# Attention and a routed feed-forward net on one core: zero products, logit sums, stores and GpSimd's multiplications in another order

## The chip, the cores and the metric

The kernel runs on one NeuronCore of a Trainium2 chip. A core has a matrix engine (TensorE, PE in the profile, with its weight loads as PEld), three engines for element-wise work (VectorE or DVE, ScalarE or ACT, GpSimd or POOL) and a queue that only issues transfers (SyncE, SP). Each engine works through its own list of instructions in order; between engines there are only waits on semaphores. TensorE writes into eight banks of PSUM, from which VectorE and ACT read. The metric is the time of one execution on the device in microseconds (us); a smaller one is better.

## The reference, cut to what matters

Sixteen sequences of 128 rows of 128 numbers attend to contexts of 77 rows (16 heads of 8). Then a net of four experts is applied four times; in each of these rounds every row is routed to its two best experts.

```python
x = x + tanh(g_xattn[0]) * xattn(layernorm(x), ctx_768, Wq, bq, Wkv, bkv, Wo, bo)
cur = layernorm(x)
for r in range(4):
    logits = cur @ Wg[r] + bg[r]
    vals, idx = top_k(logits, 2)
    cw = sum(one_hot(idx, 4) * softmax(vals)[..., None], axis=1)
    hmid = gelu(einsum('nh,ehf->enf', cur, W1) + b1[:, None, :])
    y = einsum('enf,efh->enh', hmid, W2) + b2[:, None, :]
    cur = cur + einsum('ne,enh->nh', cw, y)
x = x + tanh(g_ffn[0]) * cur
```

## The kernel before, in words

**Order.** TensorE, VectorE and ACT run in the order in which the program is written; so do GpSimd's instructions, which are pinned to it. Small lists of functions (`early`, `extra`, `behind` for each step of attention, `mid` and `post` for each piece of the experts) say between which others an instruction is put.

**PSUM.** `bank` gives one of two banks of a pool that most small products share; a new product waits until the tile that had its bank is read. `bank_tr` gives one of two others, `banks2` one of two pairs that hold the scores of a step. `warm(n)` multiplies zeros n times into a bank of `bank`; nothing reads the result.

**Attention** takes 16 steps, one for each sequence b. A step transposes the exponentials of its sequence (`turn_weights`, TensorE; ACT copies them out as `exT`), multiplies the scores of sequence b+1, has VectorE take their maximum and difference and ACT their exponential (`weights`), applies the output matrix for sequence b-1 (`put_out`, `ps_o`), takes statistics of its rows (`stats_x1`), and then (`attend`) multiplies `exT` by ones and by the values (`ps_av`) and has VectorE divide (reciprocal `rs`, product `oT`). `beats` keeps some of VectorE's instructions, so that others can be made to wait for one of them. GpSimd spreads the keys of later sequences (`km`) and norms rows.

**The rows are split in two halves** of eight tiles of 128 rows. While attention is at the second half, the first half is routed: its rows are transposed (`turned0`), the logits multiplied (`logits0`, `ps_lg`), the bias added and the gate worked out in steps (`gate0`, `gate`, one of them a Tanh on ACT), rows counted and placed (`counted0`, `routed0`, `placed0`). Then GpSimd stores the rows, tile by tile, each at its place by pair of experts (`scatter`, line 519), each store bound to one beat; SP loads them back, sorted (`load`, line 536). Line 973 says which store stands in which step.

**The turn to the experts.** In the last step `begin` copies the weights of the first four pieces (`bring`). After it stand four zero products, the transposes of the first sorted rows (`turn_half`, `ps_c`, copied to `curT`), four zero products, and the first phase, in which `put_last` finishes the last sequence.

**The experts** take eight phases: two halves in turn, four rounds. A phase has 21 pieces: two for each tile of a half, and five borders between tiles, between the fourth tile and the fifth. A piece multiplies the first layer into `ps_h`, ACT applies Gelu, and after the next piece's first layer the second layer is multiplied into `ps_y`; VectorE adds the weighted result to the rows (line 1090), and `sums` keeps these sums. VectorE also copies the weights of the piece four ahead to one of five buffers (`wb`, line 1000, 128x1028 numbers).

**The next round's routing** lies inside these phases. When a tile is finished, GpSimd multiplies its rows with the router's weights of all four experts (`multiply`, tile `lp`, four buffers), and VectorE sums (`sum_up`, line 417). In the other half's phase the last tile follows, then bias and gate up to `hot` (line 447), count (`ps_n`), places (`ps_pos`), eight stores, each bound to the latest sum of a piece, and the load. In the last two phases `finish` adds the residual to each tile and GpSimd stores it to the output (line 1098).

Of the kernel before, what the change touches and what calls it, by code (L numbers as in the profile page):

```python
# [46 lines left out]
def gated_xattn_moe(  # L47
# [358 lines left out]
    def multiply(h, r, t):  # L406

        prods[h, t] = work.tile([P, E, D], F32, tag="lp", name="lp", bufs=4)
        gp.tensor_tensor(
            prods[h, t], rows[h][:, t, 0:D].unsqueeze(1).to_broadcast([P, E, D]), wg_rows[:, r],  # L410
            ALU.mult,
        )

# [250 lines left out]
    def warm(n):  # L664

        ps = bank("ps_warm")
        for _ in range(n):
            mm(ps[:, :P], zero, zero, start=True, stop=True)
# [133 lines left out]
    def attend(b, exT):  # L802

        ps = bank("ps_av")
        for w in range(2):
            for k in range(HG):
                for g in range(NG):
                    at = slice(g * GW, (g + 1) * GW)  # L810
                    mm(
                        ps[at, ts(w, L)],
                        one[:, k, :] if w == 0
                        else vm[b // BB % 2][:, b % BB, k * D + g * GW : k * D + (g + 1) * GW],
                        exT[:, g * HG + k, :],
                        start=(k == 0),
                        stop=(k == HG - 1),
                    )
        rs = awork.tile([D, L], F32, tag="rs", name="rs")
        nc.vector.reciprocal(rs, ps[:, 0:L])  # L820
        oT = awork.tile([D, L], F32, tag="oT", name="oT")
        beats.append(nc.vector.tensor_tensor(oT, ps[:, ts(1, L)], rs, ALU.mult))
        return oT

    def put_out(b, oT, bank):
# [3 lines left out]
        nc.vector.scalar_tensor_tensor(  # L829
            row(b, D, D), ps[:, :D], tg[:, 0:1], x_sb[:, b, :],  # L830
            ALU.mult, ALU.add,
        )
# [76 lines left out]
    early = {b: [] for b in range(B)}  # L909
    behind = {b: [] for b in range(B)}  # L910
# [37 lines left out]
    def gate0(g):  # L948
        add_bg(0, 0, g, first["lg"])
        if g:  # L950
            first["gate"] = gate(0)
            advance(first["gate"], GATE_1)
# [15 lines left out]
    behind[7] += [lambda: logits0(0), lambda: gate0(0)]  # L968
    extra[9] += [lambda: turned0(1)]
    behind[9] += [lambda: logits0(1), lambda: gate0(1)]  # L970
    behind[10] += [counted0, lambda: advance(first["gate"])]
    behind[11] += [routed0, placed0, lambda: stored0(0)]
    stores_at = {(12, 0): 1, (12, 1): 2, (12, 2): 3, (13, 0): 4, (13, 1): 5, (13, 2): 6, (14, 0): 7}
# [40 lines left out]
    def begin():  # L1014
# [7 lines left out]
        junk = const.tile([1, 1], F32, name="junk")  # L1022
        nc.scalar.activation(junk, zero[0:1, 0:1], AF.Gelu_apprx_tanh)

    extra[B - 1] += [begin]
    o = {}
    for b in range(B):
# [22 lines left out]
        o[b] = attend(b, exT)  # L1050
# [4 lines left out]
        for k in range(3):  # L1055
            if (b, k) in stores_at:
                scatter(0, first["pos"], stores_at[b, k], stores, beats[n - 3 + k])
        if b == 14:
            load(0, stores)
# [51 lines left out]
    def phase(p, first_mid=()):  # L1111
# [33 lines left out]
        if ro < R:  # L1145
            s = 1 if p else 2

            if p:

                at(post, 0)(lambda: multiply(o, ro, NT - 1))  # L1150
# [74 lines left out]
        if r < R - 1:  # L1225

            for t, i, k in (
                (0, 13, 14), (1, 13, 15), (2, 14, 16), (3, 14, 17), (4, 15, 18), (5, 17, 19),  # L1230
                (6, 19, 20),
            ):
                at(post, i)(lambda t=t: multiply(h, r + 1, t))
                at(post, k)(lambda t=t: sum_up(h, t))

        for i, u in enumerate(units):
# [12 lines left out]
            def second(pc=pc, hT=hT, i=i, kind=u[0], k=u[1]):  # L1249
# [4 lines left out]
                if r == R - 1:  # L1254

                    n = i - NT - len(BORDERS)
                    if n in (0, 2, 4, 6):
                        finish(h, n // 2, id_i)
                    elif n in (1, 3, 5, 7):
                        finish(h, NT // 2 + n // 2, id_i)  # L1260
# [13 lines left out]
    warm(4)  # L1274
    turn_half(0, 0, state[0]["c"])
    warm(4)
# [36 lines left out]
```

## Time and profile before

| | us |
|---|---|
| three runs | 467.44, 467.48, 468.66 |
| their median | 467.48 |
| the profiled execution | 467.39 |
| its span in the trace | 465.60 |

| stretch of the span | from, to | length |
|---|---|---|
| start, up to the first transposes of exponentials | 0, 24.5 | 24.5 |
| attention | 24.5, 121.2 | 96.7 |
| first phase's `ps_b` to the second's | 147.12, 191.86 | 44.74 |
| each of the next five such stretches | 191.86, 395.10 | 40.64 or 40.65 |

`ps_b` is the product that brings in the second layer's bias, once in each phase; it serves as a mark.

In a row of a timeline stand the start, the length, the engine, the line of the program, the operation, what is written and from what, and the shape; "x8" means that eight instructions were merged, and a bracket at the end tells how long the engine had been idle and what ended it. A matrix product of this number type appears as two records. In a row of stretches each engine's busy time is followed by the number of its instructions in parentheses; the three last numbers are TensorE's granted clock as a share of full speed, the busy share of the transfer engines and GB/s.

### The profile page before, as it was taken

The numbers are of one execution on the slowest core, as the hardware profiler recorded it, in microseconds if no ns is written. First come the engines' busy times: TensorE is split into PE (matmuls) and PEld (weight loads), VectorE is DVE, ScalarE is ACT, GpSimd is POOL, SyncE is SP. The second block draws the span as 40 slices with busy tenths as digits, with TensorE's granted clock in tenths as the row PEclk, the third lists the DMA queues.
The fourth block names the chain that finished last, engine by engine and source line by source line (L and its number), as shares of the span: only waits on it lengthen the run. The fifth ranks groups of instructions, "written<-read, shape, count | busy, mean of one in ns | idle before, by whom it ended". The sixth has DMA issues, their size and how long they took to land.

```text
span 465.6 us, 12218 instructions
## 1 busy us (share of the span) xinstructions
PE 445.5 (96%) x4506; PEld 415.4 (89%) x4506; DVE 347.0 (75%) x900; ACT 275.0 (59%) x853; POOL 211.2 (45%) x249
## 2 busy tenths in 40 slices
PE   7999999989899899999999999999999999999991
PEld 6778888777799899999999999999999999999991
DVE  7259998989665998688579768857976885775551
ACT  2356776666555456566656656665665666566560
POOL 5354645227204732582366258236625924461042
PEclk8779999999999989999999999999999999999997
DMA  7420000002201400230121013012101301220000
GB/s 198 137 93 2 4 1 3 2 13 84 95 2 49 139 1 2 72 118 1 48 84 59 1 70 119 1 48 77 67 3 69 118 3 49 94 86 8 1 30 17
DMA packets 19553, 24.08 MB, mean 52 GB/s; under 512 B 3940, under 2 KB 16550, under 8 KB 19366
## 3 DMA queue, kind: packets, MB, share of 16 engines
q1 hardware_dynamic: 14868, 13.41, 9.1%
q0 software_dynamic: 3648, 9.71, 5.7%
q8 instruction: 36, 0.59, 0.5%
q10 hardware_dynamic: 978, 0.18, 0.2%
q14 instruction: 23, 0.19, 0.1%
HBM read 13.58 MB, written 9.71 MB: 50 GB/s over the span
## 4 chain that ended last, share of the span: by engine, by line
PE 81%; issue 7%; DVE 5%; POOL 3%; ACT 2%; POOLq 0%; DVEq 0%; ACTq 0%
PE ps_y L262 28%; PE ps_h L262 28%; PE ps_av L262 6%; PE ps_tr L265 6%; PE sc L262 2%; POOL out_dram L1098 2%; PE ps_warm L262 2%; PE ps_c L265 2%; PE ps_b L262 2%; DVE wb L1000 1%; PE ps_pos L262 1%; PE ps_o L262 1%; ACT exT L800 1%; DVE vm L197 1%; PE ps_q L262 1%
## 5 line engine op out<-in xcount | busy, mean ns | idle before, releaser
L1076 ACT ACTIVATE hT<-ps_h,wb 128x128 f32<-128x128 f32 x512 | 146.0, 368 | 87.9 <-ACT hT L1076 55.4
L262 PE MATMUL ps_h<-curT,wb 128*128 128x128 f32 x1024 | 136.3, 277 | 1.8 <-DVE wb L1000 1.8
L262 PE MATMUL ps_y<-wb,hT 128*128 128x128 f32 x1024 | 136.7, 277 | 0.0
L262 PEld LDWEIGHTS ps_h<-curT,wb 128*128 128x128 f32 x1024 | 125.5, 193 | 2.0 <-DVE wb L1000 2.0
L262 PEld LDWEIGHTS ps_y<-wb,hT 128*128 128x128 f32 x1024 | 125.4, 193 | 0.0
L519 POOL DMA_INDIRECT sorted<-rows,pos_i x64 | 69.6, 1087 | 116.5 <-DVE start L512 61.1
L1000 DVE COPY wb<-wall 128x1028 f32 x128 | 107.5, 842 | 11.7 <-issue 4.0
L93 POOL TENSOR_TENSOR lp<-rows,wg_rows 128x512 f32<-128x512 f32 x48 | 72.5, 1535 | 38.3 <-DVE rows L1090 31.4
L1090 DVE SCALAR_TENSOR_TENSOR rows<-ps_y,pws,rows 128x128 f32<-128x128 f32 x128 | 44.3, 346 | 36.2 <-PE ps_y L262 35.9
L1076 ACT ACTIVATE hT<-ps_h,wall 128x128 f32<-128x128 f32 x160 | 45.6, 368 | 35.9 <-PE ps_h L262 33.8
L800 ACT COPY exT<-ps_tr 77x512 f32<-77x512 f32 x64 | 34.1, 581 | 17.5 <-PE ps_tr L265 17.3
L262 PEld LDWEIGHTS ps_y<-wall,hT 128*128 128x128 f32 x320 | 38.9, 192 | 6.1 <-ACT hT L1076 6.1
L262 PE MATMUL ps_y<-wall,hT 128*128 128x128 f32 x320 | 43.1, 278 | 0.0
L262 PE MATMUL ps_h<-cx,wall 128*128 128x128 f32 x320 | 42.3, 275 | 0.0
L265 PEld LDWEIGHTS ps_tr<-ident,ex 128*77 128x77 f32 x256 | 29.5, 154 | 11.1 <-ACT exT L800 8.3
L262 PEld LDWEIGHTS ps_h<-cx,wall 128*128 128x128 f32 x320 | 39.0, 192 | 0.0
L265 PE MATMUL ps_tr<-ident,ex 128*77 128x128 f32 x256 | 36.8, 289 | 1.7 <-ACT exT L800 1.7
L417 DVE TENSOR_REDUCE lg<-lp 128x4 f32<-128x512 f32 x48 | 32.4, 675 | 5.5 <-POOL lp L93 5.5
L1098 POOL DMA_INDIRECT out_dram<-res,id_i x16 | 18.4, 1151 | 37.0 <-DVE res L1095 36.4
L782 DVE TENSOR_REDUCE mx<-sc 128x8 f32<-128x616 f32 x32 | 25.4, 792 | 11.8 <-PE sc L262 11.7
L792 ACT ACTIVATE ex<-ex 128x616 f32<-128x616 f32 x32 | 23.0, 719 | 10.9 <-DVE ex L786 10.4
L1090 DVE SCALAR_TENSOR_TENSOR rows<-ps_y,pwxs,rows 128x128 f32 x40 | 13.9, 348 | 17.0 <-PE ps_y L262 16.0
(162 smaller groups left out, 463.1 us busy)
## 6 DMA issues: line engine op xcount, KB each, us to landing
rows<-sorted SPq DMA_DIRECT2D x16, 528.0 KB
x_sb<-in_x_dram SPq DMA_DIRECT2D x4, 256.0 KB
wall<-in_L_ffn_W_dram SPq DMA_DIRECT2D x1, 1024.0 KB
wall<-in_L_ffn_W_dram SPq DMA_DIRECT2D x4, 256.0 KB
wg_rows<-wg_turned SPq DMA_DIRECT2D x1, 1024.0 KB
sorted<-rows,pos_i POOLq DMA_INDIRECT x64, 2.5
ctx_sb<-in_ctx_dram SPq DMA_DIRECT2D x4, 115.5 KB
out_dram<-res,id_i POOLq DMA_INDIRECT x16, 2.4
```

The costliest lines, as they stand in the source:

```text
L93: return lambda *a, **kw: tc.keep_in_program_order(f(*a, **kw))
L262: nc.tensor.matmul(*args, **kw)
L265: nc.tensor.transpose(*args)
L417: nc.vector.tensor_reduce(lgs[h][:, t, :], prods.pop((h, t)), AX.X, ALU.add)
L519: ins = nc.gpsimd.indirect_dma_start(out=sorted_rows[h], out_offset=bass.IndirectOffsetOnAxis(ap=pos_i[:, t : t + 1], axis=0), in_=rows[h] ...
L782: beats.append(nc.vector.tensor_reduce(mx, sv, AX.X, ALU.max))
L792: nc.scalar.activation(eu, eu, AF.Exp, scale=1.0 / math.sqrt(DH))
L800: nc.scalar.copy(exT[:, ts(g, HG), :].rearrange("m h l -> m (h l)"), ps[:M, :])
L1000: nc.vector.tensor_copy(wb, wall[:, ds(e, 1), :].rearrange("p o n -> p (o n)"))
L1076: nc.scalar.activation(hT[:, fc, :], ps[:, ts(fc, P)], AF.Gelu_apprx_tanh, bias=wb[:, W_B + fc : W_B + fc + 1],)
L1090: return nc.vector.scalar_tensor_tensor(at, y, w, at, ALU.mult, ALU.add)
L1098: ins = nc.gpsimd.indirect_dma_start(out=out_rows, out_offset=bass.IndirectOffsetOnAxis(ap=id_i[:, t : t + 1], axis=0), in_=res, in_offset ...
```

## The change

1. `warm` writes to a bank of the scores' pool instead of the common one.
2. `attend` is cut in two: after its products the functions of a new list `amid` run, then the division (`over_sums`). In steps 7 and 9 the routing logits and the adding of their bias are in `amid`, ahead of the division. The gate's Tanh goes from the end of step 10 to step 11, behind the copies of `exT`, and its last instruction to the end of step 11.
3. Stores of the first half: up to four in a step (VectorE's part of `put_out` becomes a beat too), so that all eight are issued by step 13, and the load one step earlier.
4. The first sorted rows are transposed in step 15 ahead of `attend`; the table for Gelu is loaded after that; the two groups of four zero products are left out.
5. Each of GpSimd's multiplications waits for the latest sum of a piece. They stand at pieces 13 to 19, one each, their sums two pieces later; the sum of the seventh tile comes in the first piece of the next phase.
6. The output stores of the last two phases stand in another order.

```diff
-    def multiply(h, r, t):
+    def multiply(h, r, t, behind):
         prods[h, t] = work.tile([P, E, D], F32, tag="lp", name="lp", bufs=4)
-        gp.tensor_tensor(
+        ins = gp.tensor_tensor(
             prods[h, t], rows[h][:, t, 0:D].unsqueeze(1).to_broadcast([P, E, D]), wg_rows[:, r],
             ALU.mult,
         )
+        after(ins, behind, "one tile for each piece of work")
...
-        ps = bank("ps_warm")
+        ps = banks2("ps_warm")
         for _ in range(n):
-            mm(ps[:, :P], zero, zero, start=True, stop=True)
+            mm(ps[:, 0, :P], zero, zero, start=True, stop=True)
...
+        return ps
+
+    def over_sums(ps):
         rs = awork.tile([D, L], F32, tag="rs", name="rs")
         nc.vector.reciprocal(rs, ps[:, 0:L])
...
-        nc.vector.scalar_tensor_tensor(
+        beats.append(nc.vector.scalar_tensor_tensor(
             row(b, D, D), ps[:, :D], tg[:, 0:1], x_sb[:, b, :],
             ALU.mult, ALU.add,
-        )
+        ))
...
-    def gate0(g):
+    def logits0_done(g):
         add_bg(0, 0, g, first["lg"])
-        if g:
-            first["gate"] = gate(0)
-            advance(first["gate"], GATE_1)
+
+    def gate0():
+        first["gate"] = gate(0)
+        advance(first["gate"], GATE_1)
...
-    behind[7] += [lambda: logits0(0), lambda: gate0(0)]
+    amid[7] += [lambda: logits0(0), lambda: logits0_done(0)]
     extra[9] += [lambda: turned0(1)]
-    behind[9] += [lambda: logits0(1), lambda: gate0(1)]
-    behind[10] += [counted0, lambda: advance(first["gate"])]
-    behind[11] += [routed0, placed0, lambda: stored0(0)]
-    stores_at = {(12, 0): 1, (12, 1): 2, (12, 2): 3, (13, 0): 4, (13, 1): 5, (13, 2): 6, (14, 0): 7}
+    amid[9] += [lambda: logits0(1), lambda: logits0_done(1)]
+    behind[9] += [gate0]
+    behind[10] += [counted0, lambda: advance(first["gate"], GATE_2 - GATE_1)]
+    extra[11] += [lambda: advance(first["gate"], 1)]
+    behind[11] += [lambda: advance(first["gate"]), routed0, placed0, lambda: stored0(0)]
+    stores_at = {
+        (12, 0): 1, (12, 1): 2, (12, 2): 3, (12, 3): 4, (13, 0): 5, (13, 1): 6, (13, 2): 7,
+    }
...
-        junk = const.tile([1, 1], F32, name="junk")
-        nc.scalar.activation(junk, zero[0:1, 0:1], AF.Gelu_apprx_tanh)
-
     extra[B - 1] += [begin]
...
-        o[b] = attend(b, exT)
+        if b == B - 1:
+            turn_half(0, 0, state[0]["c"])
+
+            junk = const.tile([1, 1], F32, name="junk")
+            nc.scalar.activation(junk, zero[0:1, 0:1], AF.Gelu_apprx_tanh)
+        ps_av = attend(b, exT)
+        for f in amid[b]:
+            f()
+        o[b] = over_sums(ps_av)
         for f in behind[b]:
             f()
 
         n = len(beats)
-        for k in range(3):
+        for k in range(4):
             if (b, k) in stores_at:
-                scatter(0, first["pos"], stores_at[b, k], stores, beats[n - 3 + k])
-        if b == 14:
+                scatter(0, first["pos"], stores_at[b, k], stores, beats[n - 4 + k])
+        if b == 13:
             load(0, stores)
...
-                at(post, 0)(lambda: multiply(o, ro, NT - 1))
+                @at(post, 0)
+                def _():
+                    multiply(o, ro, NT - 1, sums[-1])
+                    sum_up(o, NT - 2)
...
-            for t, i, k in (
-                (0, 13, 14), (1, 13, 15), (2, 14, 16), (3, 14, 17), (4, 15, 18), (5, 17, 19),
-                (6, 19, 20),
-            ):
-                at(post, i)(lambda t=t: multiply(h, r + 1, t))
-                at(post, k)(lambda t=t: sum_up(h, t))
+            for t in range(NT - 1):
+                at(post, 13 + t)(lambda t=t: multiply(h, r + 1, t, sums[-1]))
+                if t < NT - 2:
+                    at(post, 15 + t)(lambda t=t: sum_up(h, t))
...
-                    if n in (0, 2, 4, 6):
-                        finish(h, n // 2, id_i)
-                    elif n in (1, 3, 5, 7):
-                        finish(h, NT // 2 + n // 2, id_i)
+                    done = {-1: 0, 0: 1, 1: 4, 2: 2, 3: 5, 4: 3, 5: 6, 7: 7}
+                    if n in done:
+                        finish(h, done[n], id_i)
...
-    warm(4)
-    turn_half(0, 0, state[0]["c"])
-    warm(4)
     for p in range(NHALF * R):
         phase(p, () if p else (put_last, norm_last))
```

More of the change, by code (lines that the diff above doesn't have):

```diff
@@ L909, in gated_xattn_moe @@
     early = {b: [] for b in range(B)}
+    amid = {b: [] for b in range(B)}
     behind = {b: [] for b in range(B)}
```

## The prediction, made before the changed kernel was run

> **What bounds the kernel now.** I read the page's rows by engine and by slice first, then stretches cut at one mark of each phase (the start of the `ps_b` products), then the timeline where stretches differ.
>
> ```profile
> PE 445.5 (96%) x4506; PEld 415.4 (89%) x4506; DVE 347.0 (75%) x900; ACT 275.0 (59%) x853; POOL 211.2 (45%) x249
> 147.12:191.86 44.74, 42.78 (x360) 41.55 (x359) 37.02 (x88) 25.33 (x89) 19.91 (x18) 0.96 0.16 56
> 191.86:232.50 40.64, 40.64 (x359) 39.76 (x359) 31.68 (x86) 25.33 (x89) 21.25 (x17) 1.00 0.16 55
> 232.50:273.15 40.65, 40.65 (x360) 39.77 (x359) 31.72 (x86) 25.34 (x89) 21.29 (x17) 1.00 0.16 55
> ```
> From the second phase TensorE is busy all of its 40.65 us at clock 1.00: nothing can be gained there, only lost. The stretch that closes the first phase takes 44.74 with the same products: 4.09 too long. Its timeline says why:
>
> ```profile
> 155.30 0.95 POOL L519 DMA_INDIRECT sorted<-rows,pos_i  x1 [0.72 <-DVE selx L595]
> 155.73 6.04 DVE L1000 COPY wb<-wall 128x1028 f32 x1 [0.35 <-issue]
> 156.27 4.94 POOL L93 TENSOR_TENSOR lp<-rows,wg_rows 128x512 f32<-128x512 f32 x4
> ...
> 161.83 1.79 PE L262 MATMUL ps_h<-curT,wb 128*128 128x128 f32 x8 [1.84 <-DVE wb L1000]
> ```
> A weight copy of 0.70 lasts 6.04 while four of GpSimd's multiplications run without a gap; it ends 0.56 behind the last. TensorE idles 1.84 for it, then eight products take 1.79 where 0.89 is usual (clock). The rest is the way there: attention (24.5 to 121) and the turn to the experts:
>
> ```profile
> 119.26 0.86 PEld L262 LDWEIGHTS ps_av<-exT,one 77*32 77x32 f32 x32
> 121.19 1.16 PE L262 MATMUL ps_warm<-zero 128*128 128x128 f32 x8
> 122.15 0.93 DVE L820 RECIPROCAL rs<-ps_av 128x128 f32<-128x128 f32 x1
> 122.41 0.66 PE L265 MATMUL ps_c<-ident,rows 128*128 128x128 f32 x4
> 123.74 1.16 PE L262 MATMUL ps_warm<-zero 128*128 128x128 f32 x8 [0.67 <-ACT curT L379]
> 125.63 0.39 PE L262 MATMUL ps_o<-woT,oT 128*128 128x128 f32 x2
> ```
>
> **The change part by part** (a row sum is VectorE's line 1090, one for each piece; a logit sum its line 417, one for each tile), against this execution's 467.39 (span 465.60 and 1.79 around it; the median of the runs, 467.48, is 0.09 above).
>
> *Zero products in the scores' banks.* The 10 of them that start at 10.08 waited for the copy of `kT` (ACT, to 10.03). Without that they follow `ps_cols`, at about 9.6; and the two ahead of `ps_k`, which waited for ACT to 7.9 and held it up by 0.25, run at 6. From there TensorE works through to the scores, so both come off the path: 0.7. TensorE: Matmul & The Clock Gate (Part 1) has a clock that rises after a busy window of about 3.4 us. In the row, products at half clock (spacing 0.21 us) run until 15.1, and the idle 10.08 had ahead of it goes: by the rule the clock could rise one window sooner, making 2.2. Ends 0.2 and 2.2; I take 0.7, the row's. **-0.7**
>
> *Logit sums ahead of the division; Tanh later.* The view of attention:
>
> ```profile
> 71.68 1.05 PE L262 MATMUL ps_lg<-wg_sb,gT 128*128 128x4 f32 x8
> 71.82 0.96 DVE L820 RECIPROCAL rs<-ps_av 128x128 f32<-128x128 f32 x1 [0.26 <-PE ps_av L262]
> 94.00 0.23 ACT L469 ACTIVATE lg<-lg 128x32 f32<-128x32 f32 x1 [1.66 <-DVE lg L467]
> 94.75 0.91 PEld L265 LDWEIGHTS ps_tr<-ident,ex 128*77 128x77 f32 x8 [1.59 <-ACT exT L800]
> ```
> In step 7 the sum now waits for `ps_lg` (to 72.73) with reciprocal, statistics and `rstda` queued behind it on VectorE: 72.79 instead of 71.82, so GpSimd's power, then its four rows and second power (a chain without gap from 73.80 to 79.73), then VectorE's four rows of line 255 (79.76) come 1.06 late. TensorE waits there for `ps_c`: 0.8. In step 9 VectorE is late anyway (`rs` 84.88, `ps_lg` to 84.93): nothing, and `ps_xt`, which waited to 86.24, can take the bank of the sum: back 0.4. In step 11 ACT no longer stands behind VectorE's chain for Tanh: the `exT` copies start when `ps_tr` and ACT's earlier work allow, about 93.2 on the delayed timeline, not 94.14. That puts the second `ps_tr` at 93.8 instead of 94.75: 0.9 net of the 0.8. Tanh (0.23) goes behind copies that VectorE doesn't wait for; its last step (0.18) delays the positions by 0.1. Ends: -1.4 (step 7 absorbed) and +1.1 (VectorE decides step 11 too). **-0.9**
>
> *Stores four a step.* Each store takes about 0.96 and starts 0.3 behind the one before. One more in step 12 pushes `rstdf` (1.04) and the keys of step 15 (0.7; from 107.86 to about 109.1, needed at 111.39) behind it. The last then starts about 112.4, not 113.94. SP's load (issued 117.41, first half landed 120.8 by its packets) moves 1.5: landed about 119.3. Nothing else stands in SP's queue. By itself it is worth nothing; it lets the next part happen.
>
> *First rows turned in the last step.* Both groups of four zero products (1.10 and 1.16 in the chain) go; the four transposes (0.44) stand ahead of the last `ps_av`, at about 119.3, just when their rows land; `ps_av` follows at 119.75 and ends at 121.7, `ps_h` at 122.6. The curT copy (0.58) and the table load (1.28) lie beside `ps_av`. What is late next is `ps_o`: VectorE has four weight copies (to 121.43), the row, statistics, and only at 122.15 the reciprocal, unchanged; `oT` is ready at 123.40. So `ps_o` starts about 123.45 instead of 125.80 (its place in the chain), with 0.85 idle before it. Rows up to 0.4 late cost nothing; each us after that costs one. Idle of 0.85 doesn't lower the clock (1.11 before 94.75 did not). Ends -3.0 and -1.3. **-2.35**
>
> *Multiplications paced, first phase.* The second multiplication now waits for a sum on VectorE that stands behind the blocked copy, so the copy gets in behind the first: it ends about 158.1, and is needed at 159.8. The 4.09 go. Behind a waiting multiplication stand only the next ones on GpSimd, and, six pieces on, the next half's stores; only the logit sums wait for it. Here the page SBUF — State Buffer ("SBUF: two separate sides") says VectorE and GpSimd share a port pair that one instruction locks to its end. By that the copy would have lost one multiplication (1.24) and TensorE nothing, so there would be nothing to gain; the row shows it lost four. The row decides. **-4.1**
>
> *Multiplications paced, later phases.* Here the rule speaks against the change, and so does a row: where a multiplication did follow each sum, it ran first and the copy lost all of it.
>
> ```profile
> 163.62 1.27 POOL L93 TENSOR_TENSOR lp<-rows,wg_rows 128x512 f32<-128x512 f32 x1 [2.41 <-issue]
> 164.00 1.44 DVE L1000 COPY wb<-wall 128x1028 f32 x1
> 165.36 0.34 DVE L1090 SCALAR_TENSOR_TENSOR rows<-ps_y,pws,rows 128x128 f32<-128x128 f32 x1
> ...
> 300.74 0.40 DVE L447 TENSOR_TENSOR hot<-rank 128x128 f32<-128x128 f32 x1
> 301.92 0.39 PE L262 MATMUL ps_n<-ones_pp,hot 128*128 128x128 f32 x2
> ```
> From the row sum at 163.15 to the next at 165.36 are 2.21 us; a piece takes TensorE 1.786. In the later phases of before, GpSimd ran ahead and VectorE's pieces took 1.68 (copies at 284.3 to 289: 0.91). Now, in the phase shown: row sum 14 at 284.27; the multiplication starts 0.475 later, the copy asks 0.85 later (the logit sum is between) and loses. Five such pieces: row sum 19 at 295.37 (before 294.10); 2.38 for the weights' piece: 297.75; the sixth logit sum now stands ahead of the next copy, which loses to the last multiplication: 299.97; the last logit sum at 300.23, and 2.53 later, as before, `hot` ends: 302.76 instead of 301.14. `ps_n` needs it at 301.9: TensorE idles 0.9. The copy of piece 5 of that phase, the other tight one (1.1 spare), ends 1.6 later, inside that wait. Five borders (phases two to six): 4.5. At the first border GpSimd is still behind when the copy asks, pieces take about 1.7, and nothing is lost. Ends 0 (multiplications stay one behind) and 7. **+4.5**
>
> *Finishing stores reordered.* No store stands at the last but one piece, so the last starts 0.28 behind its result (456.53), at 456.8, not 457.05. **-0.25**
>
> Sum: -0.7 - 0.9 - 2.35 - 4.1 + 4.5 - 0.25 = -3.8: **463.6**.
>
> **The rivals.**
> *A: the borders stay covered.* GpSimd stays one multiplication behind, copies and multiplications take turns at 1.68 as before. For: the rows of 284 to 290. Against: the wait binds each to its own row sum. 463.6 - 4.5 = 459.1; chance 0.25.
> *B: the early half gives less.* Rows land after 120.7 and `ps_av` waits 1.0 for them, and step 7 keeps its 1.06. For: only 0.0 to 0.4 spare. 463.6 + 2.06 = 465.7; 0.13.
> *C: slower.* At each of five borders a copy loses a second multiplication (1.27), as in the first phase: 0.9 + 1.27 = 2.2 of idle each. Gains are 8.3, so from 1.7 a border the change loses; 467.39 - 8.3 + 10.9 = 470.0, more if the clock drops after such gaps, as after 1.84. Against: every multiplication now has a wait in which the copy enters. 0.07.
> *D: the first phase is not mended*: the copy loses store, multiplication and the next again. 463.6 + 4.1 = 467.7; 0.05.
>
> **How the numbers follow.** The forecast itself (borders at 0.5 to 1.3 each) has 0.50, its own range 461 to 465.9. From 459.0 (A, a little of the sooner clock) to 466.6 about 0.8 is held. What a measurement can tell from no change is about 0.3%, here 1.4 us. Faster (below 466.0): 0.47 + 0.25 + 0.09 = 0.81; within: 0.03 + 0.04 + 0.05 = 0.12; slower 0.07.
>
> **What would show it.** Stretches from `ps_b` to `ps_b`: the first 40.7, five later ones 41.5 with `ps_n` waiting 0.9 for `hot`, pairs of row sums 2.2 apart. The long copy about 2.3. `ps_o` of the last step about 2.35 sooner against the step's `ps_av`. `exT` in step 11 without Tanh ahead, VectorE's sum in step 7 waiting 0.97. If the later stretches stay 40.65, A holds and I am some 4 us high; if they exceed 42.3, C.

## The result, and the profile after

The changed kernel is slower: 469.26 us (median of 20 runs, 465.68 to 474.09) against 466.35 for the kernel before (20 runs, 465.12 to 468.66). The ratio is 1.0045, with an interval of 1.0026 to 1.0063, so about 2 us are lost (2.9 between the medians) where 3.8 were to be gained. Executions more than 1.5% above the fastest of the same kernel are called slow and stand in no ratio here, two of these 20 (473.62 and 474.09) among them; the profile of e1_again below is of such a one, so nothing rests on it alone. The prediction was wrong in its direction.

The profiled execution of the changed kernel took 465.68 us: it is the fastest of the 20. Its page begins with the engines:

```profile
PE 440.1 (95%) x4490; PEld 409.0 (88%) x4490; DVE 358.4 (77%) x900; ACT 276.4 (60%) x853; POOL 206.5 (45%) x249
```
VectorE is busy for 11.4 us more than before, although it does the same 900 instructions: those that meet one of GpSimd's last longer, as the rows below show. The stretches from one `ps_b` to the next (same columns as before the change: busy time of each engine, then clock, transfers and GB/s):

```profile
143.97:184.62 40.65, 40.65 (x360) 39.77 (x359) 33.71 (x90) 25.42 (x89) 22.24 (x17) 1.00 0.18 61
184.62:226.35 41.73, 40.88 (x360) 39.84 (x359) 34.39 (x89) 25.52 (x89) 19.69 (x17) 1.00 0.15 50
226.35:268.12 41.77, 40.89 (x360) 39.85 (x359) 34.10 (x86) 25.57 (x89) 19.70 (x17) 1.00 0.16 53
```
In this execution the first stretch is down from 44.74 to 40.65, as forecast. The five later ones are up by 1.1 each. The timeline of one of them shows the way there (VectorE, GpSimd, TensorE):

```profile
281.52 0.34 DVE L1104 SCALAR_TENSOR_TENSOR rows<-ps_y,pws,rows 128x128 f32<-128x128 f32 x1
282.00 1.27 POOL L93 TENSOR_TENSOR lp<-rows,wg_rows 128x512 f32<-128x512 f32 x1 [0.96 <-DVE rows L1104]
282.37 1.45 DVE L1009 COPY wb<-wall 128x1028 f32 x1
283.74 0.34 DVE L1104 SCALAR_TENSOR_TENSOR rows<-ps_y,pws,rows 128x128 f32<-128x128 f32 x1
...
297.97 0.46 PE L262 MATMUL ps_n<-ones_pp,hot 128*128 128x128 f32 x2 [0.88 <-DVE hot L448]
```
The multiplication starts 0.48 after the row sum that it waits for; the copy asks 0.85 after it, lasts 1.45 instead of 0.70 and ends 0.55 behind the multiplication. Row sums are 2.22 apart, `hot` is late, and TensorE stands still for 0.88. This is the mechanism of the forecast, at 1.1 a border instead of 0.9.

Attention in the same execution, step 7 to step 11:

```profile
67.10 0.17 DVE L397 TENSOR_TENSOR lg<-ps_lg,rows_b 128x16 f32<-128x16 f32 x1 [1.21 <-PE ps_lg L262]
75.14 1.97 DVE L255 TENSOR_SCALAR rows<-rows,mvf,rstdf 128x128 f32<-128x128 f32 x4 [0.95 <-POOL rstdf L93]
76.32 0.70 POOL L93 TENSOR_TENSOR km<-kT,hmask 128x308 f32<-128x308 f32 x1 [0.54 <-ACT kT L716]
77.16 0.33 PE L265 MATMUL ps_c<-ident,rows 128*128 128x128 f32 x1 [0.40 <-DVE rows L255]
83.55 1.26 POOL L93 TENSOR_TENSOR x_sb<-x_sb,bo_b 128x512 f32<-128x512 f32 x1
83.66 1.41 DVE L448 TENSOR_TENSOR hot<-rank 128x128 f32<-128x128 f32 x1
89.79 1.14 PE L265 MATMUL ps_tr<-ident,ex 128*77 128x128 f32 x8 [0.47 <-ACT exT L801]
```
The same places in the kernel before:

```profile
79.71 0.70 POOL L93 TENSOR_TENSOR km<-kT,hmask 128x308 f32<-128x308 f32 x1
79.76 1.50 DVE L255 TENSOR_SCALAR rows<-rows,mvf,rstdf 128x128 f32<-128x128 f32 x4
87.43 0.39 DVE L447 TENSOR_TENSOR hot<-rank 128x128 f32<-128x128 f32 x1
94.75 1.15 PE L265 MATMUL ps_tr<-ident,ex 128*77 128x128 f32 x8 [1.11 <-ACT exT L800]
```
The logit sum waits 1.21 for its product. The four rows of line 255 come late for it, now meet a second of GpSimd's multiplications (`km`) and last 1.97 instead of 1.50. In step 9 the gate's `hot` meets GpSimd's work on `x_sb` and lasts 1.41 instead of 0.39. In step 11 the wait for `exT` is 0.47 instead of 1.11.

And the turn to the experts:

```profile
118.10 0.60 PE L265 MATMUL ps_c<-ident,rows 128*128 128x128 f32 x4
118.63 1.08 PE L262 MATMUL ps_av<-exT,one 77*32 77x128 f32 x32
122.48 0.46 PE L262 MATMUL ps_o<-woT,oT 128*128 128x128 f32 x2 [0.58 <-DVE oT L825]
```
Here the rows are in place when TensorE comes to them, and `ps_o` waits only for the division, as the forecast had it.

Set against the kernel before, this one profile speaks for the change in most places. What it doesn't show is found by profiles of other executions.

### The profile page after: what moved, and what is told of

It is laid out like the page before. It is cut to its first block, busy times and chain, and to the rows that moved or that the text cites. A ratio compares the mean times of both kernels' runs of the same rounds, so it can differ in the third digit from the quotient of the medians.

```text
span 463.8 us, 12201 instructions
## 1 busy us (share of the span) xinstructions
PE 440.1 (95%) x4490; PEld 409.0 (88%) x4490; DVE 358.4 (77%) x900; ACT 276.4 (60%) x853; POOL 206.5 (45%) x249
## 4 chain that ended last, share of the span: by engine, by line
PE 56%; issue 15%; DVE 14%; POOL 10%; DMA 2%; ACT 1%; DVEq 1%; POOLq 0%; SPq 0%
PE ps_y L262 23%; PE ps_h L262 22%; POOL out_dram L1112 4%; DVE wb L1009 4%; POOL rows L93 2%; PE ps_warm L262 2%; DVE lg L418 2%; PE ps_b L262 2%; PE ps_tr L265 1%; DVE rows L1104 1%; PE ps_av L262 1%; PE ps_pos L262 1%; POOL km L93 1%; DMA rows<-sorted 1%; PE ps_c L265 1%
## 5 line engine op out<-in xcount | busy, mean ns | idle before, releaser
L1009 DVE COPY wb<-wall 128x1028 f32 x128 | 116.0, 908 | 12.9 <-ACT hT L1090 3.6
L520 POOL DMA_INDIRECT sorted<-rows,pos_i x64 | 69.6, 1087 | 119.0 <-DVE start L513 64.7
L93 POOL TENSOR_TENSOR lp<-rows,wg_rows 128x512 f32<-128x512 f32 x48 | 66.9, 1404 | 44.0 <-DVE rows L1104 34.5
L1104 DVE SCALAR_TENSOR_TENSOR rows<-ps_y,pws,rows 128x128 f32<-128x128 f32 x128 | 44.3, 346 | 35.4 <-PE ps_y L262 35.0
L801 ACT COPY exT<-ps_tr 77x512 f32<-77x512 f32 x64 | 34.1, 582 | 15.6 <-PE ps_tr L265 12.2
L265 PEld LDWEIGHTS ps_tr<-ident,ex 128*77 128x77 f32 x256 | 27.8, 147 | 14.0 <-ACT exT L801 9.5
L265 PE MATMUL ps_tr<-ident,ex 128*77 128x128 f32 x256 | 35.7, 281 | 3.8 <-ACT exT L801 2.4
L787 DVE TENSOR_TENSOR ex<-sc,mx 128x616 f32<-128x616 f32 x32 | 25.5, 796 | 1.5
```

What stands on the lines that cost most here:

```text
L93: return lambda *a, **kw: tc.keep_in_program_order(f(*a, **kw))
L265: nc.tensor.transpose(*args)
L520: ins = nc.gpsimd.indirect_dma_start(out=sorted_rows[h], out_offset=bass.IndirectOffsetOnAxis(ap=pos_i[:, t : t + 1], axis=0), in_=rows[h] ...
L787: nc.vector.tensor_tensor(eu.rearrange("l (g h) m -> l g h m", h=HG), sv, mx.unsqueeze(3).to_broadcast([P, 2, HG, M]), ALU.subtract,)
L801: nc.scalar.copy(exT[:, ts(g, HG), :].rearrange("m h l -> m (h l)"), ps[:M, :])
L1009: nc.vector.tensor_copy(wb, wall[:, ds(e, 1), :].rearrange("p o n -> p (o n)"))
```

## The experiments

Runs sent together (the same number behind the e) share a chip and its runs of the kernel before, and each ratio is to those; the four groups ran on four chips (which ones the first two profiles came from is not known). Every profile was cut at the same marks. This table (worked out from the traces, in us) carries most of what follows; "sc" is the product of the scores.

| run | profiled | start to 10th sc | to 14th sc | to 15th `ps_av` | to 1st `ps_b` | to 2nd | to 7th | rest |
|---|---|---|---|---|---|---|---|---|
| before | 467.39 | 73.6 | 26.9 | 13.4 | 33.2 | 44.7 | 203.2 | 70.6 |
| e3_before | 464.77 | 69.7 | 26.9 | 15.4 | 33.5 | 43.5 | 203.2 | 70.6 |
| changed kernel | 465.68 | 67.9 | 27.6 | 17.0 | 31.4 | 40.6 | 208.9 | 70.3 |
| e1_again | 471.69 | 67.9 | 27.6 | 13.4 | 37.3 | 44.5 | 208.9 | 70.3 |
| e4_again | 471.00 | 69.6 | 27.6 | 17.0 | 31.4 | 44.5 | 208.9 | 70.3 |
| e4_stores3 | 469.89 | 69.3 | 27.6 | 15.6 | 35.5 | 40.9 | 208.8 | 70.3 |
| e1_pace_only | 469.79 | 72.3 | 26.9 | 13.4 | 33.2 | 42.9 | 208.8 | 70.6 |
| e1_pace_first | 461.68 | 69.3 | 27.6 | 13.4 | 35.4 | 40.6 | 203.2 | 70.3 |
| e1_zero_only | 463.33 | 70.7 | 26.9 | 13.4 | 33.2 | 43.5 | 203.2 | 70.6 |
| e2_turn_back | 463.49 | 69.5 | 27.6 | 16.9 | 33.4 | 40.6 | 203.2 | 70.3 |
| e2_sum_back | 460.80 | 67.9 | 26.9 | 16.7 | 31.1 | 42.9 | 203.2 | 70.3 |
| e2_mix | 460.23 | 68.1 | 26.9 | 15.4 | 33.5 | 40.6 | 203.2 | 70.6 |
| e2_pace_copy | 464.31 | 69.3 | 26.9 | 15.4 | 33.5 | 41.8 | 205.0 | 70.6 |
| e3_two | 461.86 | 67.7 | 26.9 | 15.4 | 33.5 | 42.7 | 203.2 | 70.6 |
| e3_behind4 | 462.10 | 69.3 | 26.9 | 16.6 | 31.1 | 42.9 | 203.2 | 70.3 |
| e3_behind3 | 461.32 | 69.3 | 26.9 | 15.4 | 31.5 | 42.9 | 203.2 | 70.3 |

Each column has few values, and most of them go with one part of the change. A sum of parts from different executions still needs care, because the start, the stretch to the 15th `ps_av` and the one to the second `ps_b` also vary from one execution or chip to the next.

### The changed kernel twice more, the kernel before once more

> The changed kernel again. Its times lie in steps of about 1.85 us (465.7, 467.4, 469.3, 471.1). Theory (borders): the gaps of 1.1 us at the five borders sometimes bring TensorE's clock down, each time for 1.85 us; median near 469.3, and where the profiled execution is longer than 466, one or more of the stretches from ps_b to ps_b last about 43.6 instead of 41.76, with a clock below 1.00. Rival (start): the steps come from the clock in the first 30 us; then all five stretches stay 41.7 to 41.8, and the clock is below 1.00 there.

> The changed kernel a third time. Theory: five later stretches 208.9 in all once more; what makes an execution longer than 465.7 is the first border (40.65, 42.9 or 44.5), the clock before the first scores (14.9 to 16.4), and, where step 12 has no stall (13.4 instead of 17), the turn (35 to 37 instead of 31.4). Rival: a later border that is 43.6 once in the execution.

> The kernel before, unchanged, for a second profile of it. In the profiles so far the stretch from the fourteenth sc to the fifteenth ps_av lasted either 13.4 us or 15.4 to 17.0, with TensorE idle for no reason that the trace names. Theory (a trait of the chip used, not of the change): it can be 15.4 here too, and it goes with the time of the kernel before beside it. Rival (the change brings it, through what it issues or through the attention that starts sooner): 13.36 here, whatever the chip. The clock in the first 30 us: below 1.00 for about 10 us or more, as in the first profile.

The changed kernel came out at 465.77 (ratio 1.0047, 1.0022 to 1.0072) and 468.44 (1.0045, 1.0026 to 1.0064) on two occasions, and the kernel before against itself at 0.9999 (0.9982 to 1.0016). The five later stretches are 208.9 in all three profiles of the changed kernel: the borders cost 1.1 each and nothing on top, so the theory that went with e1_again, of a clock that drops there, is false. But its rival is too small: of the 5.4 us between the spans of the changed kernel's first profile and of e4_again, the start holds 1.6 and the **first border** 3.9. There, in e4_again:

```profile
153.64 0.21 DVE L601 TENSOR_TENSOR selx<-selx,act 128x48 f32<-128x48 f32 x1
153.88 1.08 POOL L520 DMA_INDIRECT sorted<-rows,pos_i  x1 [0.30 <-DVE selx L601]
154.15 0.70 DVE L1009 COPY wb<-wall 128x1028 f32 x1 [0.30 <-issue]
154.98 2.52 POOL L93 TENSOR_TENSOR lp<-rows,wg_rows 128x512 f32<-128x512 f32 x2
155.41 2.65 DVE L1009 COPY wb<-wall 128x1028 f32 x1
158.40 1.27 POOL L93 TENSOR_TENSOR lp<-rows,wg_rows 128x512 f32<-128x512 f32 x1 [0.90 <-DVE rows L1104]
158.84 1.38 DVE L1009 COPY wb<-wall 128x1028 f32 x1
...
176.50 0.47 PE L262 MATMUL ps_n<-ones_pp,hot 128*128 128x128 f32 x2 [1.62 <-DVE hot L448]
176.80 1.88 PE L262 MATMUL ps_y<-wb,hT 128*128 128x128 f32 x8
```
and in the first profile of the changed kernel:

```profile
152.06 0.21 DVE L601 TENSOR_TENSOR selx<-selx,act 128x48 f32<-128x48 f32 x1
152.18 0.96 POOL L520 DMA_INDIRECT sorted<-rows,pos_i  x1 [0.71 <-DVE selx L596]
152.62 2.38 DVE L1009 COPY wb<-wall 128x1028 f32 x1 [0.36 <-issue]
153.17 1.27 POOL L93 TENSOR_TENSOR lp<-rows,wg_rows 128x512 f32<-128x512 f32 x1
155.35 6.71 POOL L93 TENSOR_TENSOR lp<-rows,wg_rows 128x512 f32<-128x512 f32 x4 [0.90 <-DVE rows L1104]
158.33 0.91 DVE L1009 COPY wb<-wall 128x1028 f32 x1
```
Both are the same program. In the first profile the last store starts 0.12 us behind `selx`; the copy that follows lasts until the first multiplication is done (2.38), and then the engines take turns: four multiplications run without a gap, copies last 0.91. In e4_again the store starts 0.24 behind `selx`; the copy beside it takes its usual 0.70, the next one loses to two multiplications (2.65), and from there each multiplication waits 0.90 for a row sum and each copy loses to it (1.38). `hot` then comes 1.62 late, and in this execution eight products after it take 1.88 (the clock: half speed). The other profiles divide in the same way. In eleven the first phase is paced as in the diff: in five of them the store starts 0.12 or 0.13 behind `selx`, and the stretch is 40.6 to 40.9; in six it starts 0.24 or 0.25 behind, and the stretch is 42.9 or 44.5. So the pacing alone does not decide the first border; it goes with some 0.1 us in one store. What sets these was not found (the copy before differs already: 0.77 long in the early kind, as the five are called below, 0.70 in the late kind).

The kernel before has both kinds too. Its first profile is of the early one (`selx` 155.17, store 155.30, then the copy of 6.04); e3_before is of the late one:

```profile
153.70 0.21 DVE L600 TENSOR_TENSOR selx<-selx,act 128x48 f32<-128x48 f32 x1
153.95 1.08 POOL L519 DMA_INDIRECT sorted<-rows,pos_i  x1 [0.30 <-DVE selx L600]
154.21 0.70 DVE L1000 COPY wb<-wall 128x1028 f32 x1 [0.30 <-issue]
156.96 3.59 DVE L1000 COPY wb<-wall 128x1028 f32 x1
```
Its stretch is 43.5 instead of 44.7, with a stall of 1.66 at the border.

In e3_before, the kernel before has the longer stretch behind the 14th `sc` as well, and 69.7 instead of 73.6 at the start. Both are traits of the execution or the chip, and not of the change. The longer stretch is idle time of TensorE inside one group of products, for which the trace names no one:

```profile
100.03 1.06 PE L262 MATMUL ps_av<-exT,vm 77*32 77x128 f32 x20
101.39 0.43 PE L262 MATMUL ps_av<-exT,vm 77*32 77x128 f32 x5 [0.30 <-issue]
102.15 0.45 PE L262 MATMUL ps_av<-exT,vm 77*32 77x128 f32 x7 [0.32 <-issue]
```
Its cause stays open. It lies in step 12, while the first stores run.

### The pacing

e1_pace_first: in the changed kernel, the later phases as before.

```diff
-            for t in range(NT - 1):
-                at(post, 13 + t)(lambda t=t: multiply(h, r + 1, t, sums[-1]))
+            if p == 0:
+                for t in range(NT - 1):
+                    at(post, 13 + t)(lambda t=t: multiply(h, r + 1, t, sums[-1]))
...
+            else:
+                for t, i, k in (
+                    (0, 13, 14), (1, 13, 15), (2, 14, 16), (3, 14, 17), (4, 15, 18), (5, 17, 19),
+                    (6, 19, 20),
+                ):
+                    at(post, i)(lambda t=t: multiply(h, r + 1, t))
+                    at(post, k)(lambda t=t: sum_up(h, t))
```

> The changed kernel with the multiplications paced in the first phase only; the later phases issue them as before. Theory (borders): each of the five later stretches is 40.65 again, 5.5 us in all, and the steps of 1.85 go too (two in the median): 460 to 461.5, with executions within about 1 us of each other. Rival (start): 5.5 us less, 463.8, and the steps remain.

Measured: 462.01, ratio 0.9950 (0.9929 to 0.9970); on the same chip the changed kernel had 1.0047. The five stretches are 203.2. Undoing this one part turns the loss into a gain: it alone is worth 4.5 us (0.0097 of 464). The spread did not shrink (457.74 to 467.82), as the rival had it; the median lies between the two expectations.

e1_pace_only: the kernel before with the diff's pacing and nothing else.

> The kernel before with the pacing alone, in all phases. Theory (borders): first stretch 40.7 (4.1 us less), the five later ones 41.7 each (5.5 us more) and one or two drops of the clock of 1.85: 468 to 471, spread in steps of 1.85. Rival (start): 467.8, spread no wider than that of before. The prediction's own size for the borders (0.9 each): 466.8.

Measured: 469.8, ratio 1.0118 (1.0088 to 1.0149). The five stretches are 208.8 with everything else as before, so the loss belongs to the pacing. The first stretch is 42.9, not 40.7: the first border stalls for 1.61 here too, and the clock stays at 1.00 there and at all five later borders.

e2_pace_copy: the kernel before with the zero products of the change, and all multiplications paced on something else (against the change's pacing; `copies` keeps the weight copies):

```diff
-                    multiply(o, ro, NT - 1, sums[-1])
+                    multiply(o, ro, NT - 1, copies[-1])
...
-                at(post, 13 + t)(lambda t=t: multiply(h, r + 1, t, sums[-1]))
+                at(post, 13 + t)(lambda t=t: multiply(h, r + 1, t, copies[-1]))
```

> The kernel before with the zero products and with pacing in all phases, but each multiplication waits for the last weight copy instead of the last row sum. Theory (order at the shared port): a multiplication that follows a row sum starts 0.48 us after it and so ahead of the copy that asks 0.85 after it, pieces of 2.2; behind the copy it runs beside row sum and logit sum, pieces of 1.7: all stretches 40.65, 459 to 459.5, no wider than e2_mix. Rival (any pacing holds GpSimd back): five stretches of 41.7, 464.5.

Measured: 463.41, ratio 0.9955 (0.9935 to 0.9975). Neither number held: the five stretches are 205.0, 0.35 too long each, a third of the loss. In the trace a multiplication now starts earlier against the copy that follows it:

```profile
283.18 1.19 DVE L1003 COPY wb<-wall 128x1028 f32 x1
284.29 0.34 DVE L1094 SCALAR_TENSOR_TENSOR rows<-ps_y,pws,rows 128x128 f32<-128x128 f32 x1
284.50 1.28 POOL L93 TENSOR_TENSOR lp<-rows,wg_rows 128x512 f32<-128x512 f32 x1 [0.68 <-POOL lp L93]
285.14 1.19 DVE L1003 COPY wb<-wall 128x1028 f32 x1
286.25 0.34 DVE L1094 SCALAR_TENSOR_TENSOR rows<-ps_y,pws,rows 128x128 f32<-128x128 f32 x1
```
GpSimd begins 0.21 after the row sum instead of 0.48, the copy loses 0.26 less, and pieces take 1.96. The next copy asks 0.64 before the multiplication is done, and again ends 0.55 behind it. So in these two paced orders the later the multiplication starts after the row sum, the more the copy pays; the theory's 40.65 would have needed a multiplication that is done when the copy asks.

e3_two: zero products, and the first phase's multiplications at their old places but each with a wait.

```diff
-                at(post, i)(lambda t=t: multiply(h, r + 1, t))
+                at(post, i)(
+                    lambda t=t: multiply(h, r + 1, t, sums[-1] if p == 0 else None)
+                )
```

> The kernel before with zero products in the scores' banks, and the first phase's multiplications issued at the old places, two a piece, but each behind the last row sum. GpSimd then has its next multiplication at hand when one ends, yet each has a wait. Theory (the order at the port is chosen by who asks first after the wait): GpSimd stays one behind, first stretch 40.65 in nearly all executions, without the 2.2 to 3.9 us longer ones that e1_again, e1_pace_only and e2_sum_back showed in their profiles; times within 2 us of each other, as fast as the fast ones of e2_mix. Rival (four multiplications at hand starve the copy, wait or not): 44.7 again, 4 us slower than that.

Measured: 462.9, ratio 0.9924 (0.9904 to 0.9945), in six runs within 1.8 us. Neither: the first stretch is 42.7, with a store of the early kind. A copy lost 2.9 us to the last store and two multiplications (3.61 long), but not to four, and the border stalled 1.72. A wait breaks up the four; by itself it did not bring the turns.

### The zero products

e1_zero_only: the kernel before, with the zero products of the start in the scores' banks; the two groups of four ahead of the experts keep the common bank (`own` is false for them).

```diff
-        ps = bank("ps_warm")
+        ps = banks2("ps_warm")[:, 0, :] if own else bank("ps_warm")
```

> The kernel before with the zero products of the start in the scores' banks, nothing else. The prediction: 0.7 us less, 465.7. From the profile of the changed kernel, whose clock never fell in the first 30 us and whose first scores stood 3.3 us earlier, whose first ps_av 5.6 us earlier: 461 to 463, with clock 1.00 from 0 to 30 us. If the clock there is a matter of luck in each execution: a wide spread about 464.

Measured: 462.05, ratio 0.9966 (0.9954 to 0.9979), 1.6 us. The clock was not 1.00 throughout: it was at half from 7.9 to 14.7 us here, but not a second time from 22 to 29 as in the kernel before. Rows of the same stretch, the first from e1_pace_only, which has the old zero products on the same chip, the second from e1_zero_only (the clock is the third number from the end):

```profile
20.00:30.00 10.00, 9.04 (x102) 6.40 (x100) 5.88 (x10) 6.70 (x17) 4.70 (x26) 0.83 0.26 107
20.00:30.00 10.00, 8.88 (x116) 6.61 (x116) 6.96 (x13) 7.52 (x19) 4.72 (x26) 1.00 0.28 107
```
The start's length varies with and without this part (67.7 to 70.7 with, 69.7 to 73.6 without), and it goes with the time at half clock in the first 30 us. With the part it is 67.7 to 68.1 in five profiles with none, 69.3 to 69.6 in seven with 3.4 us, and 70.7 here with 6.8; without it, 69.7, 72.3 and 73.6 with 3.4, 10.2 and 13.7 us. The first profile of the kernel before was the longest of all sixteen.

### The order in attention, the stores, the turn

e2_sum_back: e1_pace_first with the division first again and the Tanh in step 10.

```diff
-    amid[7] += [lambda: logits0(0), lambda: logits0_done(0)]
+    behind[7] += [lambda: logits0(0), lambda: logits0_done(0)]
...
-    behind[10] += [counted0, lambda: advance(first["gate"], GATE_2 - GATE_1)]
-    extra[11] += [lambda: advance(first["gate"], 1)]
+    behind[10] += [counted0, lambda: advance(first["gate"])]
```

> The changed kernel with pacing in the first phase only, and the logit sums behind the division again, Tanh in one go with the rest of the gate in step 10. Theory: the sum ahead of the division costs 1.33 in step 7, gives 0.6 back in step 9 and nothing in step 11, 0.7 in all: from the tenth to the fourteenth sc 26.9 us instead of 27.6. By the end the rows' load takes it back unless the stores come sooner too: median 461.3 to 462. Rival (the prediction): the order is worth 0.9, so 462.9 here.

Measured: 460.78, ratio 0.9891 (0.9862 to 0.9920). From the tenth `sc` to the fourteenth are 26.9 as in every run with the old order; all six with the new one have 27.6. The order costs 0.7. The median is below both expectations: on this chip the turn met no wait (31.1 to the first `ps_b`, against 35.4 in e1_pace_first).

e2_turn_back: e1_pace_first with the turn, and its eight zero products, in front of the experts.

```diff
         if b == B - 1:
-            turn_half(0, 0, state[0]["c"])
...
+    warm(4, False)
+    turn_half(0, 0, state[0]["c"])
+    warm(4, False)
```

> The changed kernel with pacing in the first phase only, as in e1_pace_first, and the turn of the first rows back in front of the experts, between eight zero products. Theory (the turn meets the load): in e1_pace_first TensorE idles 1.8 us for the rows' load, in e1_again 2.5, and runs at half clock for about 7 us after it, so that from the fifteenth ps_av to the last ps_o are 13.3 and 14.5 us; here it is 11.8 as before, with clock 1.00: 1.5 us less in the profile, median 460.3 against 462.0, and a narrower spread. Rival (the prediction): the turn in the last step saves 2.35; then this is 2.35 slower, 464.4.

Measured: 464.0, ratio 0.9951 (0.9934 to 0.9969). The answer depends on the chip. This group's chip had the idle time in step 12, which gives the load some 3 us more, and there the turn in the last step is worth what was forecast: 31.1 or 31.4 to the first `ps_b` against 33.4. On the chip without it, e1_pace_first:

```profile
115.31 0.49 PE L262 MATMUL ps_o<-woT,oT 128*128 128x128 f32 x2 [0.19 <-ACT exT L802]
117.61 0.66 PE L265 MATMUL ps_c<-ident,rows 128*128 128x128 f32 x4 [1.81 <-DMA rows<-sorted]
118.20 1.94 PE L262 MATMUL ps_av<-exT,one 77*32 77x128 f32 x32
```
TensorE waits 1.81 for the load, and the clock in the seven us after it is (row of a stretch, third number from the end):

```profile
118.00:125.00 7.00, 7.00 (x82) 6.23 (x81) 2.54 (x7) 3.13 (x7) 0.00 (x0) 0.51 0.05 16
```
So `ps_av` takes 1.94 instead of 1.13, and the stretch is 35.4 instead of 33.2.

e4_stores3: the changed kernel with three stores a step and the load in its old place.

```diff
-        (12, 0): 1, (12, 1): 2, (12, 2): 3, (12, 3): 4, (13, 0): 5, (13, 1): 6, (13, 2): 7,
+        (12, 0): 1, (12, 1): 2, (12, 2): 3, (13, 0): 4, (13, 1): 5, (13, 2): 6, (14, 0): 7,
...
-        if b == 13:
+        if b == 14:
             load(0, stores)
```

> The changed kernel with three stores a step at before's places and the load behind step 14. Theory: with step 12's stall the stretch from the fourteenth sc to the fifteenth ps_av is 15.4 instead of 17.0 and the turn waits about as much longer for its rows: the same time within 1 us as e4_again. Without the stall the turn waits 2 us longer: 38 to 39 from the fifteenth ps_av to the first ps_b, 2 us slower. The prediction: by itself the fourth store is worth nothing, with the turn in the last step it is needed, so 1.5 to 2 us slower.

Measured: 470.55, ratio 1.0082 (1.0044 to 1.0120), against 1.0045 of e4_again. The intervals overlap, so the times alone don't settle it. The profile shows both halves: 15.6 instead of 17.0 behind the 14th `sc`, and then a wait of 1.82 with half clock after it, 35.5 instead of 31.4. So the four stores a step are needed for the turn: without them 4.2 are lost and 1.4 won, 2.8 in all where 1.5 to 2 were expected.

e3_behind4 and e3_behind3: e2_sum_back with the turn moved behind the last `ps_av`, with four and three stores a step.

```diff
         if b == B - 1:
-            turn_half(0, 0, state[0]["c"])
...
         ps_av = attend(b, exT)
+        if b == B - 1:
+            turn_half(0, 0, state[0]["c"])
```

> e2_sum_back with the first rows turned behind the last ps_av instead of ahead of it. Theory (the turn met the load): the last ps_av starts at once and no longer waits for the load, the rows have 2 us more, and the stretch from the fifteenth ps_av to the first ps_b is 30 to 31.5 us with clock 1.00, on a chip without the unexplained stall too, where ahead of ps_av it was 35.4 and 37.3; from the fourteenth sc to the first ps_b 44.5 without the stall. Rival: the last ps_o is set by VectorE's copies and division, and it is no better than before's 33.2.

> e3_behind4 with the stores at before's places, three a step, and the load behind step 14. Theory: without the unexplained stall the last store starts about 2.5 us later and the rows land as much later, TensorE waits about 2.5 for them: 2 us slower than e3_behind4. With the stall, which was 1.4 longer with four stores (17.0, 16.9, 16.7 against 15.4 twice), the two come out within 1 us.

Measured: 461.21, ratio **0.9877** (0.9847 to 0.9907), and 461.36, ratio 0.9892 (0.9865 to 0.9920). Both beat the kernel before beside them, and by their ratios the changed kernel too; with six runs each they can't be told apart from each other or from e2_sum_back. In e3_behind4:

```profile
120.07 0.66 PE L265 MATMUL ps_c<-ident,rows 128*128 128x128 f32 x4
121.40 1.16 PE L262 MATMUL ps_h<-curT,wb 128*128 128x128 f32 x8 [0.68 <-ACT curT L379]
```
The last `ps_av` did not wait, only the copy of the turned rows (0.68) is exposed, and the zero products are still saved. The stretch is 31.1 and 31.5. These ran on the kind of chip with the idle time in step 12; that it holds without it was not seen.

### Two parts alone

e2_mix: the kernel before, with the edits shown for e1_zero_only and e1_pace_first, that is zero products in the scores' banks and the pacing in the first phase.

> The kernel before with two parts alone: zero products in the scores' banks and pacing in the first phase. Theory: 462.05 of the zero products alone, less the 2.9 us that its first stretch was too long (43.54 against 40.65): 459.2, except in executions in which the first border stalls 1.6 us and then loses the clock (1.9). Rival: the early half of the change is worth its -3.25 (order -0.9, turn -2.35); then this is 1 to 3 slower than that, above 462.

Measured: 461.38, ratio 0.9919 (0.9882 to 0.9957); five of seven runs between 460.0 and 461.9, two at 465.5, as if the first border had stalled and lost the clock (not seen: the profile is of one of the five). The theory's 459.2 was made on a chip where the kernel before takes 463.72; that is 4.5 less, and here it is 4.65 less than 466.03. The two parts alone can't be told apart from e1_pace_first (0.9950, 0.9929 to 0.9970) with all the rest of the change.

## Why the prediction was wrong

In the order of its sum:

- **Zero products, -0.7.** Right in kind, too small: 1.6 measured, inside its ends. At the same 3.4 us of half clock the start is 0.2 to 0.5 shorter with the part. The rest goes with the second drop of the clock, at 22 us, which the sum did not have: it is in two of three profiles without the part and in none of thirteen with it. Why it stays away is not shown. The rule of the clock's windows of about 3.4 us (the Trainium skill, TensorE: Matmul & The Clock Gate, Part 1) pointed towards the other end of this term. The traces agree with it in so far as each stretch at half clock in the first 30 us is 3.41 us long or twice that.
- **Logit sums and Tanh, -0.9.** Wrong in sign: +0.7. The step that failed was to move VectorE's instructions along the timeline at their old durations. Between the same products of TensorE in both first profiles, step 7 cost 1.33 instead of 0.8, because the four rows then met a second GpSimd multiplication (1.97 instead of 1.50). Step 9 gave 0.6 instead of 0.4. But the gate's `hot` met GpSimd's work on `x_sb` (1.41 instead of 0.39), which cost 0.63 in step 10, and that took back the 0.64 that step 11 gave.
- **Stores, 0, and turn, -2.35.** The turn's gain is real (-2.1) where the rows are there. "SP's load moves 1.5" failed on the other chip: in e1_pace_first it did not move at all. Measured from the 14th `sc`, its packets start at 17.9, and so they do in the kernel before (118.43 - 100.50). The last store starts 0.75 sooner, not 1.5, and it takes 4.04 to land. In the five profiles in which no 16 KB packet of the instruction queue lies in its way it lands 2.42 to 2.44 after its start; in the eleven in which one does, after 2.87 to 4.61. So on that chip the rows came too late by 1.8, of which the packet is 1.6. "Idle of 0.85 doesn't lower the clock" was right about 0.85, but the idle was 1.8. Rival B had the late rows, at 1.0, without the clock. And four stores cost 1.2 to 1.5 in step 12's idle time, which the first profile of the kernel before did not show.
- **Pacing, first phase, -4.1.** This is the largest miss. The term was taken as certain, with 0.05 for the rival that it isn't mended, and it was sized from one execution of the early kind. There it is right: 40.65 against 44.73, and the copy lasts 2.38 where 2.3 was forecast. In the late kind the kernel before takes 43.5 and the paced one 42.9, or 44.5 where the clock drops too: 0.7 gained or 1.0 lost. Six of the eleven paced profiles are of that kind. The sentence "at the first border GpSimd is still behind when the copy asks" is true of the early kind only.
- **Pacing, later phases, +4.5.** Right in mechanism, 5.6 measured. The order of rival A, in which the engines take turns, did come with the pacing, but only at the first border of the early kind, and at none of the 25 later borders in five profiles.
- **Finishing stores, -0.25.** Right: from the seventh `ps_b` to the end are 70.33 us in all profiles with this part and 70.57 in all without.

Put together, as an estimate from these figures for a chip with the idle time in step 12: -1.6 + 0.7 + 1.4 - 2.1 + 5.6 - 0.2 = +3.8 without the first phase, which adds -4.1, -0.7 or +1.0. So the changed kernel comes out 0.3 faster, 3.1 slower or 4.8 slower, by the kind of execution; measured were some 2 slower by the ratio and 2.9 by the medians. The forecast's error is thus not one term: it used the first phase's gain at its full size from one profiled execution, and of its losses it saw the borders, but not the order in attention and the four stores. That rival C's 470.0 lies near the measured 469.26 is chance: its second lost multiplication at each border never came (1.1 lost there, not 2.2).

## What to carry to other kernels

A wait that paces one engine behind another also fixes in which order the two meet at whatever they share; if the paced instruction always arrives just ahead of the critical one, it is worse than letting it run ahead. When instructions of VectorE are moved, check what GpSimd does at their new time, since their durations are not constants. And a stretch that varies from one execution to the next can't be credited in full from one profile: take a second profile of the kernel before, ahead of forecasting a gain from the first.

## What the runs showed of the hardware

- VectorE's copies and GpSimd's multiplications hold each other up, in line with the Trainium skill's page SBUF — State Buffer ("SBUF: two separate sides"), where one instruction locks the shared ports to its end: a copy of 0.70 lasts 1.45 behind one multiplication. Which goes first varied: the same program settled into taking turns (copy 0.91, piece 1.68) or into a copy that loses each time (1.38 to 1.46, piece 2.2), and in all eleven profiles this went with the start of one earlier store, 0.12 or 0.13 us or 0.24 or 0.25 us behind an instruction of VectorE.
- An idle TensorE of 0.85 to 0.95 never lowered its clock (25 borders in five profiles). 1.60 to 1.72 at the first border did so in two profiles of nine. In front of the experts 1.81 and 1.82 did, and in the first phase of the kernel before 1.84 did; but 1.91 ahead of 8.3 us in e3_two did not. So between 1.6 and 1.9 the length alone does not decide.
- A transfer of instructions (16 KB, 0.9 to 1.6 us) can lie among a kernel's own packets and hold up the last of them, and with them whatever waits for the whole transfer. In the eleven profiles in which one fell on the last store of the first half, the last of that store's packets with rows ended 0.6 or 0.7 us after the instructions' packet.
- TensorE stood idle without a named cause in the same step, with both kernels, on some chips and not on another: the stretch is 13.4 there, 15.4 to 15.6 with three stores a step and 16.6 to 17.0 with four.
